# A pass of its own for each of the last two tile groups in layers 1 and 2 of a GraphSAGE kernel

## The chip, the cores and the metric

The kernel runs on one core of a Trainium2 chip. The metric is the device time of one execution in microseconds (us), lower is better. Five engines work side by side, each through its own queue of instructions in order: TensorE (PE; its weight loads are PEld), VectorE (DVE), ScalarE (ACT), GpSimd (POOL, which here issues the indirect gathers) and SyncE (SP, which here issues most other transfers). Sixteen DMA engines carry out the transfers of all queues.

## The reference

A graph has N = 6250 nodes with 128 features and E = 200000 edges, sorted by destination; low-numbered destinations have many more edges than high ones. A layer norm and a ReLU come first, then three layers, each of which takes for every node the maximum over its incoming edges' source rows, and two products. The widths are 128, 256, 256 on the input side and 128 at the end.

```python
def _sage_conv(x, src, dst, Wl, bl, Wr):
    agg = jax.ops.segment_max(x[src], dst, num_segments=x.shape[0])
    agg = jnp.where(jnp.isfinite(agg), agg, 0.0)
    return agg @ Wl + bl + x @ Wr
...
h = jnp.maximum(_layernorm(x, axis=-1), 0.0)
h = jax.nn.leaky_relu(_sage_conv(h, src, dst, Wl1, bl1, Wr1), 0.01)
h = jax.nn.leaky_relu(_sage_conv(h, src, dst, Wl2, bl2, Wr2), 0.01)
h = jax.nn.leaky_relu(_sage_conv(h, src, dst, Wl3, bl3, Wr3), 0.01)
return x + h
```

## The kernel before

**Tiles and groups.** The nodes are cut into 50 tiles of 127 rows. The destination tiles form four groups, k = 0 to 3: group 0 has 20 tiles of low in-degree; group 1 has 8 virtual tiles that share the edges of the three heaviest tiles (and 8 extra chunks of the same); group 2 has 8 wide tiles and 12 narrow ones; group 3 has 7 narrow ones. The code counts the layers from 0 (`layer` 0, 1, 2); the text calls them layer 1, 2, 3.

**Two ways to an edge's source row.** Most edges go over the *source pairs*: two source tiles make a pair, 25 pairs in all. For each pair `g` (from 24 down to 0) and each destination tile, at most one edge of every destination row into each of the pair's two halves (for narrow tiles: into the pair) is served by a matmul of the pair's rows with a one-hot matrix (`products`, L997), and VectorE takes the maximum of the result into the accumulator `acc` (`maxima`, L1014). Wide tiles keep the two halves apart, so a wide step has two maxima, a narrow one has one. The one-hots are made by ACT (and DVE in layer 1) from index tiles `idx_sb` (`one_hot`, L963 to L972); in layer 1 the distances that this makes are also written out (`far`), and layers 2 and 3 load them. Edges that do not fit are in *lists*, 553 rows of 128 in each layer (`Listed`): GpSimd gathers a row per partition from `table` into `g` (L1046), VectorE folds them (L1060, L1065), and the result goes to `best`.

**Node tiles.** When a destination tile's accumulator and its list are done, a `Node` fetches the list's maximum `agg` (GpSimd, L1089) and the node's own transposed rows `hT_in` (SP, L1093), transposes `agg` on PE (L1105), takes the maximum with `acc` (L1111), multiplies with both weights (L1118, L1120), and, in layers 1 and 2, writes three forms of the new row block: `table` (L1130), transposed `across` (`halves`, L872 to L875) and the pair halves `pair` (`keep_halves`, L882, L883). In layer 3 it adds `xt` and writes `out`. The stages of one node tile lie in the steps 3 to 6 after its fetch.

**Steps and the planner.** The program is written out by hand as a list of 1025 *steps*. A step is one chunk of up to 512 (layer 1: 1024) one-hot columns against one pair; layer 1 has steps 0 to 224, layer 2 225 to 624, layer 3 625 to 1024. `SWEEPS` (L1186) says which groups share a *sweep* over the 25 pairs; a sweep loads every pair once (`load_pair`, L928, L934; `PAIRS` = 4 buffers of 256 KB, that is four pairs ahead in layer 1, two in the others) and the index tiles of its groups (`load_idx`, L916 to L920; four buffers, and two of their own for group 3's). Before, with steps in brackets:

- layer 1: group 0 (0 to 74), group 1 (75 to 124), groups 2 and 3 together (125 to 224)
- layer 2: groups 0 and 1 (225 to 449), groups 2 and 3 (450 to 624)
- layer 3: groups 0 and 1 (625 to 849), group 2 (850 to 974), group 3 (975 to 1024)

The loop over the steps emits, at each, the products and maxima of the step before, one-hots for up to six steps ahead, and what an *agenda* holds for the step. The agenda is filled by a planner: the list gathers are spread evenly over the layer's steps, from the layer's start, or `rows_at` if that is later, to five before its end; a folded maximum comes 8 (layer 1) or 6 steps behind its gather, for group 3's list 4. When the layer's last sweep holds one group alone (`alone`, L1289, layer 3), the gathers are dealt in two parts: groups 0, 1, the head of group 3's list and group 2's list up to the end of group 2's sweep, the rest of group 3's list after it.

```python
t0 = max(ends_at[layer, k], done_at[k] + gap) + 1
...
t0 = max(t0, late + 1)
last = layer == 2 and k == NL - 1
every = 1 if last or layer == 0 or k in (1, 3) or ends_at[layer, k] == end else 2
...
late = t0 + every * (len(nodes) - 1)
rows_at = late + 6
```

So a group's node tiles start when its sweep and its list are done and the group before is through, every step or every second one. Before, layer 1's nodes of groups 2 and 3 are planned at steps 226 to 252, beside layer 2's first sweep, and layer 2's at 626 to 652, beside layer 3's first; `rows_at`, from which the next layer's gathers may start (they need the whole table), is 258 and 658.

Of the kernel before, what the change touches and what calls it, by code (L numbers as in the profile page):

```python
# [72 lines left out]
def kernel(ctx: ExitStack, tc: tile.TileContext, x, src, dst,  # L73
# [834 lines left out]
    def load_idx(layer, k, g):  # L908
        w = DW[k] if layer else IW[k]
        assert stored[k] == IW[k]  # L910
        if k == NL - 1:
            t = work.tile([P, DW[k]], U8, tag="idx3", name="idx_sb", bufs=IDX3)
        else:
            t = work.tile([P, max(DW)], U8, tag="idx", name="idx_sb", bufs=IDX)
        if layer:
            nc.sync.dma_start(t[:, : FW[k]], far[k][:, g, :])  # L916
            if k:
                nc.sync.dma_start(t[:, FW[k] : w], idx[k][g : g + 1, OW[k] :].partition_broadcast(P))
        else:
            nc.sync.dma_start(t[:, :w], idx[k][g : g + 1, :].partition_broadcast(P))  # L920
        idx_q[layer, k, g] = t
# [15 lines left out]
    def parts_of(k):  # L937

        units = PLANES[k]
        for w in "wnx":  # L940
            us = [i for i, u in enumerate(units) if u[0] == w]
            for i0 in range(0, len(us), HOT // P):
                yield us[i0], len(us[i0 : i0 + HOT // P]) * P
# [239 lines left out]


    steps, begins, ends_at = [], [], {}
    SWEEPS = {0: ((0,), (1,), (2, 3)), 1: ((0, 1), (2, 3)), 2: ((0, 1), (2,), (3,))}  # L1186
    sweep_of = {(layer, k): i for layer in range(3) for i, ks in enumerate(SWEEPS[layer]) for k in ks}
    for layer in range(3):
        begins.append(len(steps))
        for ks in SWEEPS[layer]:  # L1190
            for g in range(NG - 1, -1, -1):
# [90 lines left out]
    for layer in range(3):  # L1282
# [5 lines left out]
        t0, t1 = max(b0 + 2, rows_at), end - 1 - SOON  # L1288
        alone = len(SWEEPS[layer][-1]) == 1  # L1289
        items = [(k, t) for k in range(NL) for t in range(len(lists_[k].seq))]  # L1290
        if alone:
            own = [(3, t) for t in range(len(lists_[3].seq))]
            later_n = len(items) * (t1 - turn) / (t1 - t0)
            heads = [t for t, (_, j) in enumerate(lists_[3].seq) if j == 0]
            cut = min(heads, key=lambda t: abs(len(own) - t - later_n))
            mid = next(i for i, (k, _) in enumerate(items) if k == 2)
            items = items[:mid] + own[:cut] + [q for q in items if q[0] == 2] + own[cut:]
            parted = len(items) - (len(own) - cut)
# [82 lines left out]
    for i, (layer, sweep, g) in enumerate(order):  # L1381
        for k in SWEEPS[layer][sweep]:
            for c, w in parts_of(k):
# [5 lines left out]
    def load_until(i):  # L1389
        def tiles(j):  # L1390
            ks = SWEEPS[order[j][0]][order[j][1]]
            return len([k for k in ks if k < NL - 1]), len([k for k in ks if k == NL - 1])

        while loaded[0] < len(order):
# [3 lines left out]
            layer, sweep, g = order[loaded[0]]  # L1398
            for k in SWEEPS[layer][sweep]:
                load_idx(layer, k, g)  # L1400
# [37 lines left out]
    for t in range(max(max(agenda)[0] + 1, len(steps) + 1)):  # L1438
# [9 lines left out]
        if t < len(steps):  # L1448
            st = steps[t]
            layer, k, g, _ = st  # L1450
# [311 lines left out]
```

## Time and profile before

| | |
|---|---|
| median of three runs | 3156.43 us (3152.08 to 3160.95) |
| the profiled execution | 3156.75 us, its span 3155.0 us |
| busy share of the span | PE 76%, PEld 57%, DVE 80%, ACT 60%, POOL 65% |
| mean granted TensorE clock | 0.914 |
| DMA | 585.57 MB, mean 186 GB/s |
| layer 1's steps | 232 to 1162 us of the span |
| layer 2's steps | 1162 to 2117 us |
| layer 3's steps | 2117 to 3117 us |

The stretch before 232 us prepares edges and layer norm. Busy shares are averages over stages with different limits; the stages of layers 1 to 3 are best read one by one, by cutting the trace where L997's count of matmuls reaches the end of a sweep. A matmul's end is modelled, so a busy PE is not PE at its peak.

### The profile page before, as it was taken

The numbers are of one execution on the slowest core, as the hardware profiler recorded it, in microseconds if no ns is written. First come the engines' busy times: TensorE is split into PE (matmuls) and PEld (weight loads), VectorE is DVE, ScalarE is ACT, GpSimd is POOL, SyncE is SP. The second block draws the span as 40 slices with busy tenths as digits, with TensorE's granted clock in tenths as the row PEclk, the third lists the DMA queues.
The fourth block names the chain that finished last, engine by engine and source line by source line (L and its number), as shares of the span: only waits on it lengthen the run. The fifth ranks groups of instructions, "written<-read, shape, count | busy, mean of one in ns | idle before, by whom it ended". The sixth has DMA issues, their size and how long they took to land.

```text
span 3155.0 us, 36991 instructions
## 1 busy us (share of the span) xinstructions
PE 2407.1 (76%) x9909; PEld 1806.9 (57%) x9909; DVE 2523.6 (80%) x4059; ACT 1901.4 (60%) x2793; POOL 2049.3 (65%) x2059
## 2 busy tenths in 40 slices
PE   1024643568677569999987899999999996898886
PEld 1023322345455457777775677777777775676665
DVE  7576899889778666899986679995799987799854
ACT  4216963848567556666654567874666664567652
POOL 4787543667777752677776557762477777677662
PEclk9996766779888889999998999999999998999998
DMA  9224541569566657667675676766667676776684
GB/s 299 73 60 117 158 115 54 153 146 283 167 181 179 142 148 243 203 211 216 203 183 173 220 220 209 210 201 211 209 209 219 215 176 177 212 221 205 202 254 148
DMA packets 365615, 585.57 MB, mean 186 GB/s; under 512 B 64588, under 2 KB 216279, under 8 KB 364757
## 3 DMA queue, kind: packets, MB, share of 16 engines
q1 hardware_dynamic: 237141, 336.67, 33.3%
q0 software_dynamic: 84992, 212.22, 27.2%
q10 hardware_dynamic: 43264, 34.21, 3.3%
q8 instruction: 83, 1.36, 0.2%
q14 instruction: 135, 1.11, 0.1%
HBM read 458.31 MB, written 124.54 MB: 185 GB/s over the span
## 4 chain that ended last, share of the span: by engine, by line
PE 33%; DVE 26%; DMA 16%; issue 9%; POOL 7%; ACT 5%; SPq 1%; DVEq 0%; ACTq 0%; POOLq 0%
PE pg L997 25%; DVE acc L1014 11%; DMA g<-table,let 8%; POOL g L1046 6%; PE z_p L1118 3%; DVE g L1065 3%; DVE g L1060 3%; ACT away L967 2%; PE z_p L1120 2%; ACT hot L969 2%; DMA pair_sb<-pair 1%; DVE acc L560 1%; DMA hT_in<-across 1%; DVE acc L558 1%; PE hT_p L872 1%
## 5 line engine op out<-in xcount | busy, mean ns | idle before, releaser
L997 PE MATMUL pg<-hot,pair_sb 128*128 128x512 f32 x8000 | 2113.5, 416 | 383.0 <-DVE acc L1014 108.0
L1046 POOL DMA_INDIRECT g<-table,let x1659 | 1697.4, 1023 | 677.4 <-issue 383.2
L997 PEld LDWEIGHTS pg<-hot,pair_sb 128*128 128x128 f32 x8000 | 1532.9, 200 | 834.9 <-ACT hot L969 229.9
L1014 DVE TENSOR_TENSOR acc<-acc,pg 128x1024 f32<-128x1024 f32 (+2 forms) x1239 | 1434.0, 1182 | 296.0 <-PE pg L997 278.9
L969 ACT ACTIVATE hot<-away 128x1024 fp32r<-128x1024 uint8 (+2 forms) x600 | 574.1, 957 | 350.8 <-PE pg L997 338.4
L969 ACT ACTIVATE hot<-idx_sb 128x1024 fp32r<-128x1024 uint8 (+2 forms) x600 | 555.8, 937 | 232.6 <-PE pg L997 221.9
L967 ACT ACTIVATE away<-idx_sb,near 128x1024 uint8<-128x1024 uint8 (+2 forms) x600 | 620.4, 1034 | 49.9 <-DMA idx_sb<-idx 27.1
L1060 DVE TENSOR_TENSOR g<-g 128x1024 f32<-128x1024 f32 (+5 forms) x247 | 249.3, 1009 | 63.3 <-DMA g<-table,let 56.3
L1089 POOL DMA_INDIRECT agg<-best,end_i x141 | 143.1, 1015 | 213.4 <-PE aT_p L1105 146.9
L1122 ACT COPY s<-z_p 127x256 f32<-127x256 f32 (+1 forms) x150 | 50.2, 335 | 286.0 <-PE z_p L1120 236.1
L1065 DVE TENSOR_TENSOR g<-g 128x256 f32<-128x256 f32 (+3 forms) x357 | 176.9, 496 | 10.5
L1035 ACT ACTIVATE let<-ell 128x4 int32<-128x4 int16 (+3 forms) x477 | 86.5, 189 | 103.2 <-DMA ell<-picks 92.5
L1118 PE MATMUL z_p<-wr,hT_in 128*128 128x256 f32 (+1 forms) x500 | 135.6, 389 | 3.7 <-DMA hT_in<-across 3.7
L630 POOL DMA_INDIRECT picks<-picked,to_i x55 | 56.6, 1029 | 98.4 <-DVE rank_h L606 60.5
L1120 PE MATMUL z_p<-wl,mz 128*128 128x256 f32 (+1 forms) x500 | 117.2, 351 | 2.2 <-DVE mz L1111 2.1
L1111 DVE TENSOR_TENSOR mz<-acc,aT_p 128x256 f32<-128x256 f32 (+1 forms) x141 | 52.4, 372 | 81.5 <-PE aT_p L1105 81.5
L963 DVE TENSOR_SCALAR hot<-idx_sb,beyond 128x1024 fp32r<-128x1024 uint8 (+2 forms) x150 | 108.8, 725 | 0.0
L1120 PEld LDWEIGHTS z_p<-wl,mz 128*128 128x128 f32 x500 | 88.0, 202 | 12.4 <-DVE mz L1111 3.3
L1118 PEld LDWEIGHTS z_p<-wr,hT_in 128*128 128x128 f32 x500 | 80.4, 202 | 24.9 <-DMA hT_in<-across 5.3
L353 POOL DMA_INDIRECT win_d<-in_dst_dram,win_i x50 | 52.3, 1047 | 51.3 <-ACT junk_w L358 22.7
L874 ACT COPY hT<-hT_p 128x254 f32<-128x254 f32 x100 | 36.8, 368 | 72.5 <-PE hT_p L872 71.6
L1105 PE MATMUL aT_p<-ident,agg 128*128 128x128 f32 x250 | 54.4, 284 | 22.7 <-DMA agg<-best,end_i 14.2
(284 smaller groups left out, 1109.7 us busy)
## 6 DMA issues: line engine op xcount, KB each, us to landing
pair_sb<-pair SPq DMA_DIRECT2D x325, 256.0 KB
idx_sb<-far SPq DMA_DIRECT2D x50, 640.0 KB
g<-table,let POOLq DMA_INDIRECT x1659
far<-away ACTq DMA_DIRECT2D x200, 128.0 KB
pair<-pr SPq DMA_DIRECT2D x100, 256.0 KB
idx_sb<-idx SPq DMA_DIRECT2D x75, 320.0 KB
idx_sb<-far SPq DMA_DIRECT2D x50, 320.0 KB
best<-g SPq DMA_DIRECT2D x110, 128.0 KB
```

Of the source, the lines that this page charges most:

```text
L963: nc.vector.tensor_scalar(hot[:, :w], d, beyond, None, op0=OP.is_equal)
L967: nc.scalar.activation(away, d, AF.Abs, bias=near[:, s : s + 1], scale=1.0)
L969: nc.scalar.activation(hot[:, :w], d, AF.Relu, bias=1.0, scale=-1.0)
L997: nc.tensor.matmul(to, pr[:, i, kk * P : (kk + 1) * P], hot[:, o : o + bw], start=((alone or s == 0) and i == 0), stop=((alone or s == 1) ...
L1014: nc.vector.tensor_max(to, to, of)
L1035: nc.scalar.activation(let[:, :n], ell[self.k][:, q, j : j + n], AF.Identity, scale=1.0)
L1046: nc.gpsimd.indirect_dma_start(out=self.tiles[q, b][:, i, :], out_offset=None, in_=tables[self.layer], in_offset=bass.IndirectOffsetOnAxis ...
L1060: nc.vector.tensor_max(base[:, : i + 1, :], base[:, : i + 1, :], g[:, : i + 1, :])
L1065: nc.vector.tensor_max(base[:, :h, :], base[:, :h, :], base[:, w - h : w, :])
L1089: nc.gpsimd.indirect_dma_start(out=self.agg[:, : self.F], out_offset=None, in_=of, in_offset=bass.IndirectOffsetOnAxis(ap=at, axis=0),)
L1118: nc.tensor.matmul(z_p, self.hT[:, i, :], wr[layer][:, i, :], start=False, stop=False)
L1120: nc.tensor.matmul(z_p, self.m[:, i, :], wl[layer][:, i, :], start=False, stop=(i == K - 1))
```

## The change

`SWEEPS` gives groups 2 and 3 a sweep each in layers 1 and 2. The number of steps, matmuls, maxima and gathers stays; each pair is loaded once more in each of the two layers (25 of 256 KB in layer 1, 25 of 512 KB in layer 2). `alone` becomes true in layer 2, so that its gathers are dealt in two parts as in layer 3; in layer 1 it is held false, and the gathers keep their order and their steps.

```diff
-    SWEEPS = {0: ((0,), (1,), (2, 3)), 1: ((0, 1), (2, 3)), 2: ((0, 1), (2,), (3,))}
+    SWEEPS = {0: ((0,), (1,), (2,), (3,)), 1: ((0, 1), (2,), (3,)), 2: ((0, 1), (2,), (3,))}
...
         alone = len(SWEEPS[layer][-1]) == 1
         items = [(k, t) for k in range(NL) for t in range(len(lists_[k].seq))]
+        alone = alone and layer > 0
         if alone:
             own = [(3, t) for t in range(len(lists_[3].seq))]
```

By the planner's arithmetic the sweeps are then, in layer 1, group 2 at steps 125 to 199 and group 3 at 200 to 224, and in layer 2, group 2 at 450 to 574 and group 3 at 575 to 624. Group 2's 20 node tiles come at steps 201 to 220 in layer 1, one a step, and at 578 to 616 in layer 2, every second step; group 3's 7 come at 226 to 232 and 627 to 633. `rows_at` becomes 238 and 639.

## The prediction

> **What bounds the kernel now.** I first read the page's head, then cut the trace at the ends of the sweeps: L997's 8000 matmuls come in a fixed order, so counting them dates each step. Layers 1, 2, 3 are `layer` 0, 1, 2 of the code; groups are 0 to 3 as there. A step has eight matmuls (L997), in layer 1's joint sweep of groups 2 and 3 seven on average (28 in four steps).
>
> ```profile
> span 3155.0 us, 36991 instructions
> PE 2407.1 (76%) x9909; PEld 1806.9 (57%) x9909; DVE 2523.6 (80%) x4059; ACT 1901.4 (60%) x2793; POOL 2049.3 (65%) x2059
> ```
>
> No engine is full over the whole; it goes by stages. First L997 alone, then everything, in the same windows (columns: length, busy time and count of PE, of PEld, ..., the granted clock, the share of time that the DMA engines work, GB/s):
>
> ```profile
> core 0: us, PE busy (x) PEld busy (x), PEclk, DMA share, GB/s
> 660.00:755.00 95.00, 51.59 (x162) 30.88 (x160) 0.92 0.96 258
> 755.00:834.00 79.00, 60.35 (x218) 40.67 (x219) 0.96 0.79 230
> 1082.00:1162.00 80.00, 54.02 (x183) 40.63 (x184) 0.80 0.55 158
> 1162.00:1276.00 114.00, 77.17 (x268) 47.74 (x267) 0.98 0.66 214
> 1276.00:1665.00 389.00, 366.54 (x1536) 288.60 (x1534) 0.98 0.70 202
> 1665.00:1856.00 191.00, 103.47 (x364) 66.59 (x364) 0.93 0.66 206
> 1856.00:2117.00 261.00, 242.48 (x1036) 189.30 (x1036) 0.99 0.71 213
> 2117.00:2249.00 132.00, 73.88 (x263) 45.40 (x264) 1.00 0.61 198
> 2637.00:2799.00 162.00, 102.16 (x377) 69.94 (x376) 0.94 0.68 204
> 2799.00:2974.00 175.00, 155.01 (x629) 116.49 (x628) 0.98 0.64 198
> 2974.00:3117.00 143.00, 99.11 (x401) 72.27 (x399) 0.94 0.82 243
> ```
>
> ```profile
> core 0: us, PE busy (x) PEld busy (x) DVE busy (x) ACT busy (x) POOL busy (x), PEclk, DMA share, GB/s
> 1082.00:1162.00 80.00, 54.02 (x183) 40.63 (x184) 60.44 (x79) 47.26 (x61) 58.65 (x57) 0.80 0.55 158
> 1162.00:1276.00 114.00, 108.11 (x484) 78.60 (x483) 76.30 (x129) 67.16 (x128) 22.31 (x23) 0.98 0.66 214
> 1856.00:2117.00 261.00, 244.12 (x1049) 191.23 (x1048) 244.40 (x245) 205.70 (x279) 192.37 (x188) 0.99 0.71 213
> 2117.00:2249.00 132.00, 130.63 (x614) 99.97 (x615) 78.84 (x123) 66.87 (x127) 21.73 (x23) 1.00 0.61 198
> 2799.00:2974.00 175.00, 155.01 (x629) 116.49 (x628) 163.63 (x165) 129.70 (x178) 127.19 (x126) 0.98 0.64 198
> 2974.00:3117.00 143.00, 122.43 (x621) 99.27 (x619) 91.19 (x138) 68.98 (x104) 83.23 (x81) 0.94 0.82 243
> ```
>
> - Layer 2's joint sweep, past its first stretch (1856 to 2117): 1036/8 = 129.5 steps, 2.015 us each, PE and DVE both 94% busy. That is well balanced.
> - The two stretches behind a layer's end (1162 and 2117) hold 27 node tiles beside the next layer's steps. PE is 95% and 99% busy: TensorE bounds them. A node tile costs there (132 - 263/8 x 2.015)/27 = 2.43 us after layer 2, (114 - 268/8 x 2.015)/27 = 1.72 us after layer 1.
> - Layer 3 already runs what the change brings to the others, so it gives the prices. Group 2 alone (2799): 175/(629/8) = 2.226 us a step, with DVE at 164 of 175 us. Group 3 alone with group 2's nodes beside it (2974): 50 steps in 143 us, DMA share 0.82.
> - Layer 1 is paced by the gathers: in 755 to 834, without nodes, a step takes 79/(218/8) = 2.90 us. The gathers' row says why:
>
> ```profile
> L1046 POOL DMA_INDIRECT g<-table,let x1659 | 1697.4, 1023 | 677.4 <-issue 383.2
> ```
>
> One costs POOL 1.023 + 383.2/1659 = 1.254 us; layer 1 plans 509 over 218 steps, 2.33 a step or 2.93 us.
>
> **Layer 2: the joint sweep taken apart.** Before: 175 steps, 191 + 261 = 452 us. The first stretch (1665 to 1856, nodes of groups 0 and 1) is 191 - 364/8 x 2.015 = 99 us over the quiet rate; these nodes keep their steps, so I keep the 99 (layer 3's like stretch, with cheaper nodes, is 162 - 377/8 x 2.226 = 57 over: I estimate that the excess can move by some 15 us either way).
>
> After, group 2 alone: of its five steps two are wide, and a wide step has two maxima, so 7 maxima on 5 steps where the joint sweep has 9 on 7. VectorE gains the bound. At layer 3's rate 125 x 2.226 + 99 = 377 us.
>
> Group 3 alone: layer 3's 143 us, but its node tiles are dearer in layer 2. PE work of a node: (130.63 - 73.88)/27 = 2.10 us in layer 2, (122.43 - 99.11)/20 = 1.17 in layer 3. If the difference falls on the path, 143 + 20 x 0.93 = 162 us. Below: PE's work alone, 99 + 20 x 2.10 = 141. Above, by bytes:
>
> ```profile
> pair_sb<-pair SPq DMA_DIRECT2D x325, 256.0 KB
> pair<-pr SPq DMA_DIRECT2D x100, 256.0 KB
> table<-h SPq DMA_DIRECT2D x100, 128.0 KB
> across<-hT SPq DMA_DIRECT2D x100, 128.0 KB
> hT_in<-across SPq DMA_DIRECT2D x100, 128.0 KB
> xt<-in_x_dram SPq DMA_DIRECT2D x49, 56.0 KB
> out_dram<-s SPq DMA_DIRECT2D x49, 56.0 KB
> ```
>
> A node moves its aggregate and `hT_in` (128 KB each) in both layers; in layer 2 also a table row block, `across` and half a pair (512 KB), in layer 3 `xt` and `out` (some 127 KB with their small rests): 385 KB more, 20 times, 7.9 MB. Layer 3's pass moved 143 x 243 = 34.7 MB; 42.6 MB at 258 GB/s (the row with the engines 96% busy) take 165 us, at 243 GB/s 175. I take 162, nearest to the rows for PE and for bytes, and keep 141 and 175.
>
> What the 27 -> 7 nodes save behind layer 2's end: 20 x 2.43 = 49 us. Layer 2: 377 + 162 - 452 - 49 = **+38 us** (+17 to +51 by the group 3 pass alone). The separate pass also loads 25 more pairs of 512 KB; they are inside layer 3's 143 us, where they are the longest link:
>
> ```profile
> 2984.47 5.90 DMA pair_sb<-pair
> 3002.43 5.15 DMA pair_sb<-pair
> 3034.10 6.82 DMA pair_sb<-pair
> ```
>
> ```profile
> PE pg L997 <- DMA pair_sb<-pair: 15.3, 10, 3.9
> ```
>
> (First three pieces of the chain of waits: start, length. Then PE's waits for a pair: us, times, longest.) Next to this, TensorE's granted clock is 0.94, against 0.99 in the joint sweep. The Trainium skill, "TensorE: Matmul & The Clock Gate", section "HAM oscillation — how this bites in real kernels", speaks against such a pass: idle gaps of over some 3.4 us put the clock to half. The row agrees in direction only; 0.94 is far from half, and its cost stands inside the 143. Held at half clock throughout, PE's 141 us would become an estimated 282, some 120 us more on the sum.
>
> **Layer 1.** There `alone` is switched off, so the gathers keep their order and rate; group 2's list is done in step 180, and its 20 nodes come in steps 201 to 220, one a step, beside group 3's pass. The nearest row is 660 to 755, where group 0's 20 nodes run one a step beside gathers: 162/8 = 20.25 steps, 4.69 us each, DMA engines 96% busy. POOL alone would need (2.33 + 1) x 1.254 = 4.18 us. The pass: 20 x 4.69 + 5 x 2.90 = 108 us. Before, the last 25 steps took 25 x 80/(183/7) = 77 us. So +31, and 20 x 1.72 = 34 saved behind the layer's end: **-3 us**. Ends: -34, if PE's idle 26 of 80 us took the nodes (20 x (108.11 - 77.17)/27 = 23 us) for nothing; +20, if each step, which now needs its own pair and its own index tile of two buffers, takes 1.2 us more.
>
> **Gathers start earlier.** With 7 nodes left, layer 2's gathers begin in step 238 instead of 258, layer 3's in 639 instead of 658: 553 over 362 steps, 1.53 a step, become 477 over 331 (the rest later), 1.44. In the quiet part of layer 2 the chain goes through gathers too:
>
> ```profile
> by line: PE pg L997 43.6%; DVE acc L1014 15.7%; DMA g<-table,let 13.6%; POOL g L1046 9.5%; issue 8.4%; DVE g L1065 3.7%; DVE g L1060 3.6%; ACT hot L969 1.7%; DVEq L1060 0.2%; DVEq L1065 0.1%; DVEq L1014 0.0%; ACT let L1035 0.0%; POOLq L1046
> ```
>
> 13.6 + 9.5 + 8.4 = 31% of 389 us, 5.5% less: 6.6 us in each of the two layers, **-13 us**; between 0 (PE bounds: 366.54 of 389) and -43 (gathers set the whole pace).
>
> Nothing else moves: the added pair and index loads stand on SP's queue behind the nodes' stores, which is in the prices above; POOL's moved fetches stand among the gathers.
>
> **Sum:** -3 + 38 - 13 = +22 us. The profiled execution took 3156.75 us (its span 3155.0), the median of the runs 3156.43: they agree, and I forecast 3178 us. About 0.3% (9.5 us) is what a measurement of this kernel can tell from no change.
>
> **Rivals.**
>
> *The transfers hide (faster).* If the pair loads of a pass come in time, layer 2's group 3 pass costs PE's 141 us and layer 1's nodes are nearly free (-25), and the gathers' relief reaches -30: -25 + 17 - 30 = -38, 3118 us. For it: the DMA engines are at 0.82 in layer 3's pass, not full, and PE idles in layer 1. Against it: the 5 to 7 us pieces above, and 0.96 in the 4.69 us steps. The Trainium skill, "DMA: Bandwidth & Descriptors", section "Specifications", gives about 358 GB/s for one core's HBM traffic; by it 42.6 MB take an estimated 119 us, under PE's 141. The trace disagrees: 258 GB/s at 0.96. Chance 0.2.
>
> *Load, steps and node in series (much slower).* SP issues in order, so a pair's load can stand behind a node's store that waits for this step's results. Then each of the 20 pairs of steps with a node costs about 5 us of load (the pieces) and 2.10 for the node and 2 x 99.11/50 for the matmuls, 11.1 us, the other five 9: 266 us, and layer 1 its +20: 3157 + 22 + 104 + 23 = 3306 at the worst; half of the excess, some 3240, is likelier, as four buffers hold two source pairs. It decides from the point where a load takes longer than one pair's steps. Chance 0.15.
>
> *It does not do what it says.* If group 2's lists ended with the layer, its nodes could not move. By the planner they end at steps 180 and 574, before group 2's passes do at 200 and 575; only a longer delay could undo it, at about +87 in layer 2 and nothing saved. Chance 0.05.
>
> **How the numbers follow.** Forecast 0.6, with its own range 3150 to 3215 (the ends above, not all at once). The rivals beside it stretch this to 3130 and 3240. Faster: the first rival and a tenth of the forecast's low end, 0.24; same 0.13; slower 0.63.
>
> **What would show it.** Right: group 2's pass in layer 2 at 2.2 us a step with DVE over 90%, group 3's at 3.0 to 3.4 with pair loads in the chain, both stretches behind a layer's end only 7 nodes long, layer 1's last 25 steps at over 4 us with the DMA share over 0.9. Wrong: group 3's pass in layer 2 at 2.8 us or less, layer 1's at about 3 us, or the steps between nodes and group 2's pass well under 2.0.

## The result and the profile after

The change makes no difference that can be measured: 3157.59 us (median of 12 runs, 3150.42 to 3167.12) against 3157.09 us (12 runs, 3146.63 to 3162.85), ratio 1.0005 with a 95% interval of [0.9992, 1.0018]. The forecast was 3178 us, slower. Several of the later runs fell on chips on which the kernel before itself takes 3650 to 3707 us; they are called the slower chips here, though it is not shown that the chip makes the difference. Each ratio is taken against the kernel before, run beside it, and times of the two kinds are not compared.

L997 in the profile of the changed kernel, cut at the ends of its sweeps (length in us, PE busy and count, PEld, granted clock, DMA share, GB/s; a step is eight matmuls in all of these windows):

```profile
core 0: us, PE busy (x) PEld busy (x), PEclk, DMA share, GB/s
1079.00:1204.00 125.00, 58.17 (x203) 39.45 (x202) 0.85 0.81 248
1204.00:1280.00 76.00, 65.86 (x266) 48.99 (x266) 0.99 0.74 206
1280.00:1657.00 377.00, 362.27 (x1537) 284.60 (x1536) 1.00 0.71 203
1657.00:1860.00 203.00, 115.81 (x398) 74.18 (x398) 0.92 0.69 212
1860.00:2020.00 160.00, 147.47 (x602) 108.77 (x601) 1.00 0.65 201
2020.00:2191.00 171.00, 101.49 (x405) 72.16 (x404) 0.95 0.86 266
2191.00:2270.00 79.00, 64.33 (x264) 47.95 (x264) 1.00 0.63 186
2270.00:2651.00 381.00, 363.64 (x1540) 288.11 (x1539) 0.99 0.70 203
2819.00:2981.00 162.00, 147.99 (x601) 109.98 (x600) 0.99 0.64 199
2981.00:3118.00 137.00, 97.44 (x398) 70.54 (x397) 0.98 0.85 253
```

Three windows of the kernel before that the prediction did not show, layer 3's first sweep, layer 2's joint sweep from step 500 on and layer 3's group 2 from step 900 on:

```profile
2249.00:2637.00 388.00, 365.13 (x1538) 286.37 (x1537) 0.99 0.73 206
1866.00:2118.00 252.00, 234.58 (x1004) 183.12 (x1003) 0.99 0.71 212
2807.00:2974.00 167.00, 148.16 (x600) 111.23 (x599) 0.98 0.64 200
```

Both kernels were profiled a second time later (the runs "before again" and "changed again" below). Stage by stage, in us, with both profiles of each:

| steps | stage | before | changed | forecast | measured |
|---|---|---|---|---|---|
| 0 to 199 | layer 1 up to group 3's pass | 853, 855 | 849, 850 | 0 | -4 |
| 200 to 224 | layer 1's last 25 steps | 77, 77 | 124, 126 | +31 | +48 |
| 225 to 257 | behind layer 1's end | 113, 112 | 76, 77 | -34 | -37 |
| 258 to 449 | layer 2's first sweep | 389, 392 | 377, 376 | -7 | -14 |
| 450 to 624 | layer 2's groups 2 and 3 | 452, 453 | 534, 521 | +87 | +75 |
| 625 to 657 | behind layer 2's end | 132, 132 | 80, 81 | -49 | -51 |
| 658 to 849 | layer 3's first sweep | 388, 386 | 380, 377 | -7 | -8 |
| 850 to 974 | layer 3's group 2 | 337, 342 | 331, 334 | 0 | -7 |
| 975 to 1024 | layer 3's group 3 | 142, 135 | 136, 143 | 0 | +1 |

A stage repeats within some 3 us, the passes of group 3 alone, which wait for transfers, and the stretches with node tiles at a pass's start within 8. So group 3's two passes cost more than was forecast (125 us where 108 was, 171 and 165 where 162 was), the stretches behind the layers' ends gave back what was forecast, and the stages with list gathers gave more: the first sweeps, and group 2's pass in layer 2 (364 and 356 us where 377 was). The level total is a balance of terms of up to 75 us, not a sign that nothing moved. The rest is the test of these three readings.

### The profile page after: what moved, and what is told of

Its sections match the earlier page's. It is cut to its first block, busy times and chain, and to the rows that moved or that the text cites. A ratio compares the mean times of both kernels' runs of the same rounds, so it can differ in the third digit from the quotient of the medians.

```text
span 3156.4 us, 37156 instructions
## 1 busy us (share of the span) xinstructions
PE 2406.2 (76%) x9909; PEld 1794.7 (57%) x9909; DVE 2522.3 (80%) x4059; ACT 1903.9 (60%) x2793; POOL 2048.5 (65%) x2059
## 5 line engine op out<-in xcount | busy, mean ns | idle before, releaser
L997 PE MATMUL pg<-hot,pair_sb 128*128 128x512 f32 (+1 forms) x8000 | 2107.2, 414 | 350.8 <-ACT hot L969 107.4
L997 PEld LDWEIGHTS pg<-hot,pair_sb 128*128 128x128 f32 x8000 | 1520.5, 198 | 809.9 <-ACT hot L969 236.2
L1014 DVE TENSOR_TENSOR acc<-acc,pg 128x1024 f32<-128x1024 f32 (+3 forms) x1239 | 1435.1, 1182 | 327.4 <-PE pg L997 309.4
L967 ACT ACTIVATE away<-idx_sb,near 128x1024 uint8<-128x1024 uint8 (+2 forms) x600 | 620.6, 1034 | 54.5 <-DMA idx_sb<-idx 29.8
L1118 PE MATMUL z_p<-wr,hT_in 128*128 128x256 f32 (+1 forms) x500 | 136.6, 391 | 0.0
L1120 PE MATMUL z_p<-wl,mz 128*128 128x256 f32 (+1 forms) x500 | 119.5, 356 | 3.6 <-DVE mz L1111 3.6
L963 DVE TENSOR_SCALAR hot<-idx_sb,beyond 128x1024 fp32r<-128x1024 uint8 (+1 forms) x150 | 108.2, 721 | 3.3 <-DMA idx_sb<-idx 3.3
L1120 PEld LDWEIGHTS z_p<-wl,mz 128*128 128x128 f32 x500 | 89.7, 205 | 14.2 <-DVE mz L1111 4.9
L1118 PEld LDWEIGHTS z_p<-wr,hT_in 128*128 128x128 f32 x500 | 80.5, 202 | 23.0 <-DMA hT_in<-across 3.1
L872 PE MATMUL hT_p<-ident,h 128*128 128x128 f32 x200 | 42.3, 294 | 52.9 <-DVE mz L1111 33.5
```

The costliest lines, as they stand in the source:

```text
L963: nc.vector.tensor_scalar(hot[:, :w], d, beyond, None, op0=OP.is_equal)
L967: nc.scalar.activation(away, d, AF.Abs, bias=near[:, s : s + 1], scale=1.0)
L997: nc.tensor.matmul(to, pr[:, i, kk * P : (kk + 1) * P], hot[:, o : o + bw], start=((alone or s == 0) and i == 0), stop=((alone or s == 1) ...
L1014: nc.vector.tensor_max(to, to, of)
L1118: nc.tensor.matmul(z_p, self.hT[:, i, :], wr[layer][:, i, :], start=False, stop=False)
L1120: nc.tensor.matmul(z_p, self.m[:, i, :], wl[layer][:, i, :], start=False, stop=(i == K - 1))
```

## The experiments

**The kernels themselves, once more.** No edit.

> The kernel before itself, for its stages on this chip. Its last 25 steps of layer 1 76 us and the stretches behind the layers' ends 113 and 132 us, as in its first profile; its first sweeps of layers 2 and 3, with 1.53 gathers a step, some 470 and 465 us (A), like those of the changed kernel with late gathers.

> The changed kernel itself, once more, on a chip on which the kernel before takes some 3650 us (with the stretches without gathers as long as before and those with gathers 15 to 20% longer). Theory A, thinner gathers pay: where gathers cost more, the change gains more; its first sweeps of layers 2 and 3 take some 450 and 430 us (late gathers: 471 and 461), group 2's passes past the node tiles 180 to 185 (late gathers: 196 and 197); total 0.985 to 0.995 of the kernel before. Rival B, thinner gathers do nothing and late gathers only moved other work: 470 and 460 us, total 1.000 to 1.005.

These two expectations were written for a slower chip; the runs fell on one where the kernel before takes 3161 us. The changed kernel: 3156.65 us, ratio 0.9991 [0.9979, 1.0003]; the kernel before: one run, 3153.22 us. Their stages stand in the table. With the first result this makes the change level twice.

**Late gathers.** The changed kernel with the gathers of layers 2 and 3 as dense as before: 1.53 a step instead of 1.44.

```diff
-        rows_at = late + 6
+        rows_at = late + 6 + (20, 19, 0)[layer]
```

> The changed kernel with the gathers of layers 2 and 3 held back to steps 258 and 658, for a chip on which the kernel before takes some 3157 us. Theory A, thinner gathers bring the gain that the forecast lacked: first sweeps of layers 2 and 3 some 389 us (changed kernel: 377 and 380), group 2's passes past the node tiles 165 to 168 us (changed: 160 and 162), in all +25 to +35 us against the changed kernel, ratio to the kernel before 1.007 to 1.010. Rival B, they got quicker by what else the change moved: stages within 3 us of the changed kernel's, ratio 0.998 to 1.002. At the forecast's own price (+13) the ratio is 1.003 to 1.004.

3186.47 us, ratio 1.0091 [1.0074, 1.0109]: some 29 us above the changed kernel, by theory A, and more than twice the forecast's price of 13. The profiled run, 3194.70 us, is the slowest of its six, so its stages may read a few us too long. Its windows for layer 2's first sweep, group 2's pass past step 500, layer 3's first sweep and group 2's pass past step 900:

```profile
1286.00:1668.00 382.00, 365.06 (x1537) 287.31 (x1537) 0.99 0.74 203
1872.00:2039.00 167.00, 148.09 (x600) 111.22 (x599) 0.98 0.64 200
...
2288.00:2671.00 383.00, 363.46 (x1537) 286.21 (x1538) 0.99 0.75 202
2844.00:3014.00 170.00, 151.12 (x602) 114.11 (x601) 0.96 0.64 196
```

Against the changed kernel's 377, 160, 381 and 162 us (in its second profile 376, 160, 377 and 162) that is +5 or 6, +7, +2 to 6 and +8. The expectation of 389 us for the first sweeps failed: they went back by about half only. So of their gain (14 and 8 us) some 5 us each come from the thinner gathers, the rest from something else in the change. One candidate is that no node tiles run into the sweep's start while the gathers begin. The nodes left behind (next experiment), with the same dense gathers but all 27 node tiles behind the ends again, have these sweeps at 385 and 390 us against 382 and 383 here: 3 and 7 us that way, from one profile of each, and so borne out in part only. Group 2's passes, where the forecast had put no gain at all, are the clearest: 7 and 8 us of 168.

The same kernel ran twice on slower chips, under this expectation both times:

> The changed kernel, but the list gathers of layers 2 and 3 may not start before steps 258 and 658, as in the kernel before (the changed kernel starts them at 238 and 639). Theory A, the gathers' relief was mis-sized: with 1.53 gathers a step again, the quiet part of layer 2's and layer 3's first sweeps (1.96 and 1.98 us a step in the changed kernel) goes back to 2.02, and group 2's own passes (2.13 and 2.16 us a step past step 500 and 900) to 2.2; in all +25 to +45 us against the changed kernel. Rival B, the passes and first sweeps got quicker for another reason (node tiles gone from the start of the sweep, TensorE's clock): the steps stay at 1.96 to 1.98 and 2.13 to 2.16, and the total moves by less than 8 us. The price of the forecast itself would be +13.

3671.68 us, ratio 1.0036 [1.0012, 1.0059], and 3662.07 us, ratio 1.0044 [1.0007, 1.0082]. The stage times in the text are those of a faster chip and cannot be held against them, and the changed kernel itself was not run there. On slower chips the density counts for more: layer 3's first sweep with dense gathers (late gathers; then separate passes in layer 1 alone) and with thin ones (three index tiles, below), all on slower chips:

```profile
2596.00:3059.00 463.00, 395.55 (x1538) 300.39 (x1538) 0.92 0.62 170
```

```profile
2606.00:3077.00 471.00, 390.86 (x1539) 296.31 (x1538) 0.93 0.61 171
```

```profile
2603.00:3036.00 433.00, 383.79 (x1538) 296.77 (x1537) 0.94 0.62 175
```

The last two ran side by side: 38 us for 1.44 instead of 1.53 gathers a step. Two more pairs that ran side by side give 26 us (separate passes in layer 1 alone with early biases, 463, against layer 2 alone, 437) and 39 us (late gathers, 463, against early biases, 424).

**The nodes left behind.** The changed kernel, group 2's node tiles planned behind the layer's end as before (steps 226 and 626 on, one a step), so that each pass of group 3 stands alone.

```diff
-            t0 = max(ends_at[layer, k], done_at[k] + gap) + 1
+            t0 = max(end if layer < 2 else ends_at[layer, k], done_at[k] + gap) + 1 if k == 2 else max(ends_at[layer, k], done_at[k] + gap) + 1
...
-            every = 1 if last or layer == 0 or k in (1, 3) or ends_at[layer, k] == end else 2
+            every = 1 if last or layer == 0 or k in (1, 3) or ends_at[layer, k] == end or k == 2 and layer < 2 else 2
```

> The changed kernel, but group 2's node tiles of layers 1 and 2 stay behind the layer's end (steps 226 and 626 on), as before; the gathers start at 258 and 658 again. A (the pass itself is dear in layer 2, the nodes come nearly free beside it; in layer 1 it is the nodes): layer 2's group 3 pass some 130 to 145 us for its 50 steps, held by its pair loads, so the passes lose 40 us and more; layer 1's last 25 steps some 75 to 85 us; total 1.010 to 1.020 of the kernel before. Rival B (the passes are free by themselves, the nodes alone make them long): layer 2's pass 100 to 110 us, total 1.000 to 1.005.

3207.38 us, ratio 1.0150 [1.0128, 1.0171]. Layer 1's last 25 steps, group 2's pass past step 500, group 3's pass of layer 2, and the stretch behind it:

```profile
1077.00:1163.00 86.00, 53.85 (x201) 41.21 (x199) 0.88 0.75 209
1865.00:2035.00 170.00, 151.10 (x601) 113.88 (x600) 0.96 0.63 196
2035.00:2159.00 124.00, 94.23 (x401) 78.85 (x399) 0.89 0.81 243
2159.00:2292.00 133.00, 75.33 (x263) 46.45 (x264) 0.99 0.61 196
```

Neither end of the expectation: 124 us lie between 100 to 110 and 130 to 145, layer 1's 86 just above its 75 to 85; the total is A's. The passes by themselves cost 170 + 124 = 294 us where the joint sweep took 252 for the same steps (500 to 624): +42. What holds group 3's pass is told by its chain of waits:

```profile
by line: PE pg L997 49.6%; DMA pair_sb<-pair 38.6%; DMA idx_sb<-far 3.4%; issue 3.2%; DVE g L1060 1.0%; DVE g L1065 0.9%; ACT hot L969 0.8%; ACT away L967 0.7%; SPq L918 0.7%; SPq L1069 0.5%; ACT let L1035 0.3%; DVEq L1060 0.1%; ACTq L1035 
```

Two fifths of it are pair loads. With the 20 node tiles beside it the pass takes 165 to 170 us, 2.0 to 2.3 us more for each, about their 2.10 us of PE work; behind the layer's end they cost 51 us, 2.6 each. So the node tiles were not hidden, they only got some 0.4 us cheaper. That kills the rival in which the transfers hide and the nodes come free. The chain of the same pass with the node tiles in it is on record for the late gathers (166 us):

```profile
by line: PE pg L997 22.8%; issue 12.1%; PE z_p L1118 12.0%; DMA pair<-pr 9.9%; PE z_p L1120 9.7%; DMA pair_sb<-pair 9.2%; PE hT_p L872 4.8%; DVE h L1129 4.5%; DVE mz L1111 3.5%; DMA idx_sb<-far 2.8%; PE z_p L1116 2.2%; DVE g L1060 1.9%; DVE
```

The node tiles' work on PE (L1118, L1120, L872, L1116) is 29% of it, their pair stores (`pair<-pr`) another 10%. So both are on the path, TensorE's work for the most part.

**One layer alone.** The separate passes in layer 2 alone, and in layer 1 alone:

```diff
+    SWEEPS = {0: ((0,), (1,), (2, 3)), 1: ((0, 1), (2,), (3,)), 2: ((0, 1), (2,), (3,))}
```

```diff
+    SWEEPS = {0: ((0,), (1,), (2,), (3,)), 1: ((0, 1), (2, 3)), 2: ((0, 1), (2,), (3,))}
```

> The separate passes in layer 2 alone. Where the kernel before takes some 3157 us: A (the stages add up): up to step 450 as before, 450 to 658 +24 to +32 us, layer 3 -10 to -15: +10 to +20 us, ratio 1.003 to 1.006. Rival: level or faster, if layer 2's passes pay by themselves. Where the kernel before takes some 3650 us: 0.99 to 1.00, as in its run there.

3167.12 us, ratio 1.0036 [1.0022, 1.0051]. Steps 500 to 574, 575 to 624, 625 to 657, and layer 3's first sweep:

```profile
1860.00:2028.00 168.00, 149.18 (x603) 111.65 (x602) 0.98 0.65 199
2028.00:2193.00 165.00, 101.64 (x402) 72.49 (x400) 0.97 0.90 275
2193.00:2275.00 82.00, 66.56 (x264) 49.24 (x264) 0.98 0.65 181
2275.00:2654.00 379.00, 361.72 (x1537) 286.85 (x1538) 0.99 0.72 204
```

From step 500 up to step 658 that is 415 us, before 384; from step 658 on it takes 847 us, before 865 and 867, so layer 3 gives back some 19. Layer 2's passes lose, as expected, by 10 us. With dense gathers in layer 2 its group 2 pass is at 168 us again. On a slower chip the same kernel wins:

> Only layer 2 has the two separate passes; layer 1 as before, layer 2's gathers from step 258. Theory A (terms add up, thinner gathers bring what the changed kernel showed): up to step 450 as before; group 2's pass somewhat slower than in the changed kernel, as its gathers are denser (1.53 a step); steps 450 to 658 +32 to +42 us against the kernel before; layer 3 quicker by 15 to 20 through its earlier gathers; slower in all by +0.4 to +0.8%. Rival B (thinner gathers do nothing): steps 450 to 658 +29, layer 3 unchanged, slower by 0.9%.

3634.11 us, ratio 0.9937 [0.9898, 0.9977]; the expected loss did not come. That layer 3's gathers are the reason is argued from its first sweep (437 us, above), not tested on its own.

Layer 1 alone ran three times, always on slower chips:

> Only layer 1 has the two separate passes; layer 2 keeps the joint sweep of groups 2 and 3, but its gathers start at step 238 instead of 258. Theory A (terms add up): layer 1 and the stretch behind it as in the changed kernel (+6 us against the kernel before, up to step 258), layer 2's sweeps quicker by the thinner gathers (-12 in the first, some -5 in the joint one), layer 3 as before: -8 to -14 us in all. Rival B (no relief from thinner gathers): +6 us.

> The separate passes in layer 1 alone, for a chip on which the kernel before takes some 3157 us. Terms add up (A): layer 1 and the stretch behind it +6 us, the first sweep of layer 2 -14 and its joint sweep some -5 (thinner gathers), layer 3 as before: -10 to -16 us, ratio 0.995 to 0.997. Rival B, the gain in layers 2 and 3 needs the passes of layer 2: +6 us, ratio 1.001 to 1.003.

> The separate passes in layer 1 alone, biases late. A (the stages add up): some 10 us above the run with early biases as well (0.9933), -8 to -14 us against the kernel before, ratio 0.9955 to 0.9975. Rival: without the early biases the passes of layer 1 bring nothing, 0.999 to 1.001.

3648.72 us, ratio 0.9990 [0.9959, 1.0020]; 3699.66 us, 0.9990 [0.9958, 1.0021]; 3645.89 us, 1.0001 [0.9968, 1.0034]. Level each time; what it gives on a faster chip is left to the next experiment, where it stands with one more edit.

**Early biases.** In the changed kernel layer 1's last step takes 17 us (17.05 and 17.2 in its two profiles). DVE around it (start, length, instruction, idle before and what ended it):

```profile
1185.55 1.09 DVE L1014 TENSOR_TENSOR acc<-acc,pg 128x896 f32<-128x896 f32 x1 [0.42 <-PE pg L997]
1196.62 0.28 DVE L806 CAST b_parts<-b 1x256 bf16<-1x256 f32 x1 [9.98 <-DMA b<-in_L_gnn_bl_dram]
...
1201.69 0.22 DVE L806 CAST b_parts<-b 1x128 bf16<-1x128 f32 x1 [3.57 <-DMA b<-in_L_gnn_bl_dram]
...
1202.71 0.40 DVE L1129 SCALAR_TENSOR_TENSOR h<-s 127x256 f32<-127x256 f32 x1
```

`load_layer` for layers 2 and 3 stands at layer 1's end. Its bias loads are queued on SP behind the node tiles' stores and the loads of layer 2's first pair, DVE waits for them in order, and behind DVE the node tiles and TensorE, whose next instruction is a node tile's transpose:

```profile
1203.26 0.66 PE L872 MATMUL hT_p<-ident,h 128*128 128x128 f32 x2 [14.85 <-DVE h L1129]
```

In the kernel before the same waits of DVE were 1.13 and 3.80 us. In the nodes left behind, where no node tile's store stands ahead of the bias, DVE still waits 7.08 us for the first one:

```profile
1162.50 0.28 DVE L806 CAST b_parts<-b 1x256 bf16<-1x256 f32 x1 [1.13 <-DMA b<-in_L_gnn_bl_dram]
1167.79 0.21 DVE L806 CAST b_parts<-b 1x128 bf16<-1x128 f32 x1 [3.80 <-DMA b<-in_L_gnn_bl_dram]
```

```profile
1165.34 0.28 DVE L806 CAST b_parts<-b 1x256 bf16<-1x256 f32 x1 [7.08 <-DMA b<-in_L_gnn_bl_dram]
```

(First the kernel before, then the nodes left behind.) There two loads of layer 2's first pair (3.15 us on SP) stand ahead of the bias, which in the kernel before did not; yet the last step takes only 5.6 us, with no node tile's transpose there for TensorE to wait at. So the stores are only a part of the delay, and it is dear where a node tile stands behind it. The edit loads the biases first and splits them in the preparation (shortened):

```diff
+    raw = []
+    for i, b in enumerate((bl1, bl2, bl3)):
+        raw.append(first.tile([1, b.shape[0]], F32, name=f"raw{i + 1}"))
+        nc.sync.dma_start(raw[i], b.rearrange("(o f) -> o f", o=1))
...
     load_layer(0, const, first)
+    for i in range(3):
+        split_bias(i, const, first)
```

> The changed kernel with the three biases loaded and split in the preparation, for a chip on which the kernel before takes some 3157 us. If DVE's wait for the biases made the last step of layer 1's group 3 pass 17 us long: that step goes to about 4 us, the pass from 124 to 111, the total to 0.995 to 0.997 of the kernel before. Rival: something else of that place is as late (weights, layer 2's first pairs): the pass stays above 120 us, ratio 0.998 to 1.001.

3143.01 us, ratio 0.9963 [0.9951, 0.9975]. The last step takes 6.2 us instead of 17, the 25 steps 115, 10 us less (4 and 111 were expected):

```profile
1084.00:1199.00 115.00, 58.22 (x201) 39.73 (x199) 0.89 0.85 256
```

On a slower chip:

> The changed kernel, with the three biases loaded and split at the start (in the preparation) instead of at layer 1's end, where DVE stands still until the biases have come in behind the node tiles' stores. If that wait is what made the last step of layer 1's group 3 pass 17 us long (TensorE idle 14.9 us in one piece): that step goes to about 4 us, the total by -9 to -14 us. Rival: another transfer of the same place (weights, layer 2's first pairs) is just as late, and the step stays above 12 us: total within 4 us.

3596.86 us, ratio 0.9840 [0.9769, 0.9911], of four runs and with a wide interval; there the thin gathers of both layers are likely to add to it.

The same edit on the kernel before:

> The kernel before with the biases split early, nothing else. A: DVE's waits for the biases at layer 1's end were 1.1 and 3.8 us there and TensorE stood still for 2.9 us only, so -3 to -6 us, ratio 0.998 to 0.999; the separate passes in layer 1 with early biases (0.9933) owe the rest to the passes. Rival: the biases alone bring 0.994 or less in any kernel, and the passes nothing.

3154.19 us, ratio 0.9994 [0.9982, 1.0006]: nothing that can be measured in the total, though the stretch behind layer 1's end went from 113 to 105 us in its profile. The stall of 15 us is the change's own; a smaller one, which the total cannot tell from nothing, was there before.

**Layer 1 alone with early biases.** Both edits above.

> The separate passes in layer 1 alone and the biases split early. Where the kernel before takes some 3157 us: A (the stages add up: layer 2's passes cost 24 us up to step 658 and bring layer 3 some 14): 3130 to 3136 us, below the changed kernel with early biases (3143). Rival: layer 3's thinner gathers are worth more than layer 2's passes cost: 3143 or above. Where the kernel before takes some 3650 us, thinner gathers are worth more than twice as much, and it is level with the kernel before.

3136.32 us, ratio 0.9933 [0.9917, 0.9949]: the fastest, faster than both kernels, by theory A. Layer 1's last 25 steps, the stretch behind, layer 2's first sweep and the quiet part of its joint one (steps 500 to 624):

```profile
1081.00:1197.00 116.00, 57.15 (x202) 39.03 (x201) 0.91 0.83 256
1197.00:1273.00 76.00, 66.84 (x264) 49.30 (x264) 0.97 0.79 217
1273.00:1643.00 370.00, 359.20 (x1538) 284.24 (x1539) 1.00 0.71 206
1845.00:2099.00 254.00, 234.17 (x1003) 184.61 (x1002) 0.99 0.69 204
```

Steps 200 to 257 take 192 us, before 190: moving the node tiles into layer 1's pass is level. The gain lies in layer 2's first sweep, 20 us, whose gathers start 20 steps earlier with no passes to pay for. Late gathers put only some 5 us of such a sweep's gain down to the gathers, so the rest stays unexplained here too. The joint sweep, expected to gain too, did not (254 against 252). On slower chips:

> Early biases (as in the kernel with that name) and the separate passes in layer 1 alone; layer 2 keeps its joint sweep. Theory A, the terms add up: against the kernel before, layer 1 and what lies behind it -6 to -8 us, layer 2's sweeps -12 to -17 by the thinner gathers, layer 3 as before: faster by 0.5 to 0.8%. Rival B: the early biases alone make a kernel faster and the passes nothing: as fast as the changed kernel with early biases.

> The separate passes in layer 1 alone and the biases split early. A: some 10 to 14 us below the run with the separate passes in layer 1 alone, 3130 to 3135 us, ratio 0.991 to 0.993, and so below the changed kernel with early biases (3143). Rival: layer 3's thinner gathers, which this kernel gives up, are worth more than the passes of layer 2 cost, and it comes out at 3143 or above.

3643.05 us, ratio 0.9979 [0.9951, 1.0006], and 3701.94 us, 0.9997 [0.9971, 1.0022]: level, and short of the gain that both expectations named. There the changed kernel with early biases is the better one.

**Three index tiles.** The changed kernel with three buffers for group 3's index tiles (`IDX3 = 3`), on a slower chip.

> The changed kernel with three buffers instead of two for group 3's index tiles. A (the pass is held by transfers and gathers as a whole: 20 steps at 4.69 us in the forecast): layer 1's last 25 steps stay at 120 us or more, total within 4 us of the changed kernel. Rival B (held by waiting for the next index tile): the 25 steps go to 105 us or less, and layer 2's group 3 pass also gets a little shorter; total -15 us.

3595.19 us, ratio 0.9879 [0.9835, 0.9922]. Layer 1's last 25 steps:

```profile
1277.00:1402.00 125.00, 55.70 (x202) 37.37 (x200) 0.87 0.80 239
```

125 us; with two buffers and late biases the same 25 steps take 122 to 133 us in five profiles on slower chips. ScalarE's waits for index tiles (L967) in these steps are 5.6 us in all, against 19.4 us in the second late-gathers trace from a slower chip, and the pass did not get shorter: it is not held by the number of their buffers (A). The changed kernel was not run on this chip; how much of the ratio is the edit's stays open.

## Why the prediction was wrong

Point by point, by its own steps:

- *Layer 2's group 2 pass, 377 us.* Measured 364 and 356. The rate of 2.226 us a step was read off layer 3 with 1.53 gathers a step and carried over to a pass with 1.44. Late gathers shows the difference: 2.23 with dense gathers, 2.13 with thin ones. Here the step failed that carried the rate over; it accounts for some 11 of the 17 us, the rest is open.
- *Layer 2's group 3 pass, 162 us.* Measured 170 and 165: right, slightly low, and inside the ends 141 and 175. That a node tile beside the pass costs about its PE work is shown by the nodes left behind (124 us without them), and the chain with them in it has that work as 29%. The Trainium skill, "TensorE: Matmul & The Clock Gate", section "HAM oscillation — how this bites in real kernels", lets idle gaps of over some 3.4 us put the clock to half. The prediction held 0.94 against it as far from half. That reading is wrong: the clock records of these traces hold only 1 and 0.5, and a pass's mean is a mixture. In the nodes left behind the pass's 0.89 over 124 us is some 27 us at half; behind TensorE's longest wait for a pair, and in the changed kernel behind the 14.85 us of the biases, the windows show it plainly:

```profile
2144.79 7.49 PE L997 MATMUL pg<-hot,pair_sb 128*128 128x512 f32 x26 [9.15 <-DMA pair_sb<-pair]
2139.00:2148.00 9.00, 3.21 (x8) 2.56 (x9) 0.50 0.67 252
```

```profile
1193.00:1206.00 13.00, 2.43 (x6) 2.01 (x7) 0.50 0.48 151
```

So direction and size agree here; the half clock holds for about a fifth of the pass, and what it cost by itself was not measured.
- *Behind the ends, -34 and -49.* Measured -37 and -51: right.
- *Layer 1's pass, +31.* Measured +48. The row taken for it, 4.69 us a step, was nearly right: with the biases loaded early the 25 steps take 115 us where 108 was forecast. The sign named for it was not met: the DMA share was to be over 0.9 and is 0.81, or 0.85 with early biases. What was missed is one wait, 10 of the 17 us: the biases of the next layers, for which DVE waited 1.13 and 3.80 us in the trace of before and 9.98 and 3.57 after. The step that failed is "nothing else moves": it looked at the loads that the change adds, but not at the small loads that stayed and now stood behind them. The other 7 us are open.
- *Gathers start earlier, -13.* This is the term that was mis-sized: late gathers shows 29 us. I had multiplied the gathers' share of one sweep's chain (31%) with 5.5% and applied it to the two first sweeps alone. The thinner gathers also speed up the passes of group 2 (7 and 8 us), where VectorE, which folds the gathers, is the busiest engine (153 of 160 us), and by a few us the stretches between. Which part of a gather it is that costs (POOL's issue, the landing or the fold) was not tested.

Put together: -16 in the gathers' term (29 instead of 13), of which some 11 stand in layer 2's group 2 pass, -4 up to step 199, -3 and -2 behind the ends, and some -13 in the first sweeps and -6 in layer 2's group 2 pass that the thin gathers do not explain, against +17 in layer 1's pass and +5 in layer 2's group 3 pass; the stages' sum is +2 where the forecast had +22. So the gathers' term is the largest miss that an experiment shows, and nearly as much again, in the same stages, is seen but not explained. That the total came out level to 0.05% is the balance of these misses, and no step of the prediction gave it. That layer 2's passes lose was right: alone they cost 10 us. Of the rivals, the first (the transfers hide) has fallen, and its half about the gathers' relief of 30 us is what came true; the second, with 266 us for layer 2's group 3 pass, has fallen too (171 and 165), as has the third, since the node tiles did move.

## What to carry to other kernels

A change that lets a background stream (here the gathers) start earlier thins it over all the stages behind; price it in each stage by a run with the stream held back, not by its share in one chain. A rate read off one stage holds for another only with the same background load. When work is moved into a place, list what already waits there in order, however small: a load of 1 KB that came late through its place in a queue cost the pass 10 us, and moving it made the difference between level and faster. Read a granted clock in short windows before holding it against a rule: the mean of a pass hides stretches at half.

## What the runs showed of the hardware that was not expected

The same kernel has two speeds, and they differ in the stages with gathers. The kernel before took 3157 us in some places and 3650 to 3707 us in others. What makes a place slow is not known: the record's chip numbers 0 and 8 stand with both speeds, so it need not be the chip. The stretch behind layer 2's end, which has no gathers, took the same on both kinds; here the kernel with separate passes in layer 1 alone on a slower chip:

```profile
2475.00:2606.00 131.00, 73.42 (x263) 44.97 (x262) 1.00 0.63 198
```

131 us there, 132 before. The first sweep of layer 3, with dense gathers in it, took 388 us on the one and 459 to 484 on the other. The trace of the slower chips shows ScalarE and VectorE idle for some 350 and 330 us in all (layer 1 alone, its first run) in some 70 and 100 waits that no recorded engine ends, which the faster chips' traces do not have; what they wait for was not found. It turns the ranking round: on the slower chips the kernels with thin gathers in both layers 2 and 3 are the fastest (ratios 0.984 and 0.988), on the others the one that thins layer 2's alone (0.9933).
